# Turning the mixture's tokens and slot rows with VectorE and SBUF transfers instead of TensorE, and three PSUM copies on ScalarE

## The chip, the cores and the metric

The kernel runs on one core of a Trainium2 chip. A core has TensorE (PE in the profile; its weight loads are PEld), VectorE (DVE), ScalarE (ACT), GpSimd (POOL) and SyncE (SP), which here only starts transfers. Each engine works through its own list of instructions in order and waits on semaphores for the others. TensorE reads SBUF and writes PSUM, which has eight banks of 128 x 512 float32. The metric is the device time of one execution in microseconds; lower is better.

## The reference, cut to what matters

Tokens `x` of shape (2, 1024, 256), all in float32, pass four blocks, each added to `x`, with a parameterless layer norm in front:

```python
x = x + _L0_xattn_ref(_layernorm(x), ctx, Wq, Wk, Wv, Wo, bo)      # 8 heads, windowed, 64 context rows
x = x + _L0_ffn_ref(_layernorm(x), W1, b1, W2, b2)                 # 8 groups of tokens, no activation
x = x + _L1_xattn_ref(_layernorm(x), ctx, ctx, Wq, Wk, Wv, Wo)     # 16 heads, sigmoid scores
x = x + _L1_ffn_ref(_layernorm(x), gamma_x, gamma_slot, slot_embeds, w1, w2)
```

The last is a soft mixture with 1,024 slots. It is the part that most of the change touches:

```python
xn = rms_norm(x, gamma_x)
se = rms_norm(slot_embeds, gamma_slot)
logits = einsum('bsd,etd->bset', xn, se)
dispatch = softmax(logits, axis=1)          # over the tokens
slots = einsum('bsd,bset->betd', xn, dispatch)
processed = gelu(slots @ w1) @ w2
combine = softmax(logits over all slots)
out = einsum('bnd,bsn->bsd', processed, combine)
```

For the logits, both tokens and slot rows must lie with the 256 features on the partitions, that is, turned.

## The kernel before, in words

**Tiling.** The 2,048 tokens are four quads (`q` 0 to 3) of 512, each 4 tiles (`t`) of 128 tokens by 256 features, kept in SBUF as `xq[q]`. Quads 0 and 1 are sequence 0, quads 2 and 3 sequence 1. The 256 features are two halves of 128 (`c`, `dc`).

**Order.** The order on each engine is set at compile time: a scheduler reorders the program's instructions by its own estimates, and only the mixture's ScalarE instructions keep the written order. PSUM is two pools of four banks (`bank(name, side)`); a new bank waits until the one four earlier in its pool has been read out. So an instruction that reads a bank late can hold up TensorE four banks on.

**Layer 0** (L596 to L813). `weigh(q)` computes attention weights on VectorE and ScalarE, `attend(q)` turns them (`pat`, L760), copies them out of PSUM to `atT` (L762, on an engine that the compiler chooses) and multiplies (`po`, L767); VectorE adds that to `x` (L775). The feed-forward block has no activation, so `product(g)` multiplies its two weight matrices (`pmt`, L522), and `bias_rows(g)` sums the biases on VectorE, for `g` from 2 on as eight instructions of 128x256 (`b2z`, L553). `bias(g)` makes `bs` from them (`pbs`, L559; copied by L561), which GpSimd adds to `x` (L574); `norm_ff` and `feed_forward` finish (`hn_f` L486, `pt_f` L125, `hT_f` L126, `po` L580, L587).

**Layer 1** (L815 to L1006). Keys are masked by head parity out of PSUM bank `pk` (L862, VectorE), values copied from `pv` (L875, L885, VectorE). Then for each quad and each half `c` of the heads: scores (`psg`, L957), tanh on ScalarE (`sg`, L966), values (`poT`, L996; read out to `oT` by L1003). Between scores and values stands other work that hides ScalarE: the norm of the next quad (`hn_a` L486, turned by `pt_a` L125), its queries (`pq`, L897), and the output of the quad before (`pf`, L911; added to `x` by VectorE, L919).

**Mixture, preparation.** `norm_slots` scales the 1,024 slot rows `se`: squares on ScalarE (L826), the power on GpSimd (L829), three small steps on VectorE, and eight scalings on VectorE (L834). `turn_slot_rows(dc, h)` turns them on TensorE (`pse`, L842, four transposes each); VectorE copies them to `seT` and multiplies by both gammas on the way (L843). `norm_tokens(q)` computes moments (L113, L114), `rstd` and `f` (GpSimd L116, L117, L159, then six small VectorE steps L160 to L165) and `xh` (L169). `turn_tokens(q)` turns `xh` on TensorE (`pt_m`, L180, eight transposes), read out by ScalarE and VectorE (L150, L152) to `xhT`. `norm_tokens(0)` and `turn_tokens(0)` stand near the end of layer 1, the others among the logits.

**Mixture, logits and after** (L1012 on). For each row tile, `logits` multiplies `xhT` by `seT` (`pl`, L196); VectorE reads each 128x512 half twice (L204 for the negated logits and their minimum, L211 or L215 for the running maximum over tokens), ScalarE takes the exponential (L219). `largest` and `spread` bring the maxima to all partitions (`pm`, `pb`), GpSimd adds them (L278), ScalarE takes the second exponential (L281), and `gather`, `hidden`, `processed` and `combine` follow (L289, L364, L430, L455). `turn` (L228) already turns the combine weights `ec` without TensorE: VectorE turns 32x32 blocks (L236) and 16 transfers per piece (L243), issued by SP, put the blocks in their places.

Of the kernel before, what the change touches and what calls it, by code (L numbers as in the profile page):

```python
# [9 lines left out]
FP = mybir.dt.float32  # L10
AF = mybir.ActivationFunctionType
ALU = mybir.AluOpType
# [3 lines left out]
P = 128  # L16
B = 2
S = 1024
D = 256
DC = D // P  # L20
NK = 64
QT = 4
# [28 lines left out]
def tile_kernel(  # L51
# [9 lines left out]
    bo0: bass.AP,  # L61
    wff_in: bass.AP,
    b2: bass.AP,
    gammas: bass.AP,
    w1_in: bass.AP,
    slots_in: bass.AP,
# [12 lines left out]
    def bank(name, side=0):  # L79
        return ps[side].tile([P, 512], FP, tag="bank", name=name)  # L80
# [11 lines left out]
    nc.gpsimd.memset(m_half, -0.5)  # L92
    xq = [const.tile([P, QT, D], FP, name=f"x{q}") for q in range(NQ)]

    gxs = const.tile([P, 2, DC], FP, name="gxs")
    gx, gs = gxs[:, 0, :], gxs[:, 1, :]
    ggx = const.tile([P, DC], FP, name="ggx")

    parity = const.tile([P, 2], FP, name="parity")
    nc.vector.tensor_reduce(  # L100
# [2 lines left out]
        AX.XY,  # L103
        ALU.add,
    )
    seT = const.tile([P, DC, NSLOT], FP, tag="seT", name="seT")

    def moments(xt, name):

# [10 lines left out]
    def transposed(src, dst, name, side=0):  # L120

        for c in range(DC):
            pt = bank(f"pt_{name}_{c}", side)
            for t in range(QT):
                nc.tensor.transpose(pt[:, ts(t, P)], src[:, t, ts(c, P)], ident)  # L125
            nc.any.tensor_copy(dst[:, c, :], pt)  # L126


    outr = out.rearrange("(q t p) d -> q p t d", t=QT, p=P)
# [43 lines left out]
        xhs[q] = xh  # L173

    def turn_tokens(q):
        xhT = pools["mw"].tile([P, DC, QN], FP, tag="xhT", name=f"xhT_{q}", bufs=2)
        for c in range(DC):
            pt = bank(f"pt_m_{q}_{c}", 1)
            for t in range(QT):
                nc.tensor.transpose(pt[:, ts(t, P)], xhs[q][:, t, ts(c, P)], ident)  # L180
            copy(c, xhT[:, c, :], pt)
        xhTs[q] = xhT

    def logits(b, s):

        q, t = b * QB + s // QT, s % QT
        if s == 0:
            zcs[b] = stat.tile([P, ST], FP, tag="zc", name=f"zc_{b}")
            rmaxs[b] = pools["md"].tile([P, NSLOT], FP, tag="rmax", name=f"rmax_{b}")
        lg = keep[b].tile([P, NSLOT], FP, tag=f"lg_{s}", name=f"lg_{b}_{s}")  # L190
        lgs[b][s] = lg
        nm = stat.tile([P, 2], FP, tag="nm", name=f"nm_{b}_{s}")
        for n in range(NSLOT // 512):
            pl = bank(f"pl_{b}_{s}_{n}", 0)
            for dc in range(DC):
                nc.tensor.matmul(  # L196
                    pl,
                    lhsT=xhTs[q][:, dc, ts(t, P)],
                    rhs=seT[:, dc, ts(n, 512)],
                    start=(dc == 0),  # L200
                    stop=(dc == DC - 1),
                )

            nc.vector.tensor_tensor_reduce(  # L204
                lg[:, ts(n, 512)], pl, zero.to_broadcast([P, 512]), -1.0,
                BIG if n == 0 else nm[:, 0:1], ALU.add, ALU.min, nm[:, n : n + 1],
            )

            rm = rmaxs[b][:, ts(n, 512)]
            if s == 1:  # L210
                nc.vector.scalar_tensor_tensor(  # L211
                    rm, lgs[b][0][:, ts(n, 512)], -1.0, pl, ALU.mult, ALU.max
                )
            elif s > 1:
# [253 lines left out]
    with (  # L468
# [4 lines left out]
        wk1s, wv1s, wq1s, wo1s = (w1s[:, i] for i in range(4))  # L473
        se = w1p.tile([P, EC, D], FP, name="se")

        NCT, NPE = DC * 2 * B * NK, DC * NK
        fr = w1p.tile([P, NCT + NPE + NG * OC], FP, name="fr")
        ctxd = fr[:, 0:NCT].rearrange("p (c b e s) -> p c b e s", c=DC, b=B, e=2)
# [112 lines left out]
        def load_layer1():  # L591
            nc.sync.dma_start(out=w1s, in_=w1_in)
            nc.sync.dma_start(out=se, in_=slots_in)
            nc.sync.dma_start(out=gxs, in_=gammas)

        with tc.tile_pool(name="p0", bufs=1) as p0, tc.tile_pool(name="a0", bufs=2) as a0:  # L596

# [158 lines left out]
            def attend(q):  # L756
                atf = ats[q].rearrange("p g j -> p (g j)")
                pat = bank(f"pat_{q}")
                for t in range(QT):
                    nc.tensor.transpose(pat[:, ts(t, P)], atf[:, ts(t, P)], ident)  # L760
                atT = a0.tile([P, QN], FP, tag="atT", name=f"atT_{q}")
                nc.any.tensor_copy(atT, pat)  # L762
                for i in range(2):
                    po = bank(f"po0_{q}_{i}")
                    for k in range(2):
                        t = 2 * i + k
                        nc.tensor.matmul(  # L767
                            po[:, ts(k, D)],
                            lhsT=atT[:, ts(t, P)],
                            rhs=vw[:, (q * QT + t) // 2, :],  # L770
                            start=True,
                            stop=True,
                        )
# [41 lines left out]
        with (  # L815
# [4 lines left out]
            def norm_slots():  # L820
                sq = a1c.tile([P, D], FP, name="sq")
                sn = a1c.tile([P, EC], FP, name="sn")
                p_half8 = a1c.tile([P, EC], FP, name="p_half8")
                nc.gpsimd.memset(p_half8, 0.5)
                for c in range(EC):
                    nc.scalar.activation(  # L826
                        sq, se[:, c, :], AF.Square, accum_out=sn[:, c : c + 1]
                    )
                nc.gpsimd.tensor_tensor(sn, sn, p_half8, ALU.pow)  # L829
                nc.vector.tensor_scalar(sn, sn, RMS_EPS, None, ALU.max)  # L830
                nc.vector.reciprocal(sn, sn)
                nc.vector.tensor_scalar(sn, sn, float(D) ** 0.5, None, ALU.mult)
                for c in range(EC):
                    nc.vector.tensor_scalar(  # L834
                        se[:, c, :], se[:, c, :], sn[:, c : c + 1], None, ALU.mult
                    )
                nc.vector.tensor_tensor(ggx, gx, gs, ALU.mult)

            def turn_slot_rows(dc, h):
                pt = bank(f"pse_{dc}_{h}", 1)  # L840
                for c in range(4):
                    nc.tensor.transpose(pt[:, ts(c, P)], se[:, 4 * h + c, ts(dc, P)], ident)  # L842
                nc.vector.tensor_scalar(  # L843
                    seT[:, dc, ts(h, 512)], pt, ggx[:, dc : dc + 1], None, ALU.mult
                )

# [12 lines left out]
                    )  # L859
            for c in range(C1):  # L860
                for e in range(2):
                    nc.vector.tensor_scalar(  # L862
                        kblk[:, c, :, e, :],
                        pk[:, ts(c, P)].rearrange("p (b s) -> p b s", b=B),
                        parity[:, e : e + 1],
                        None,
                        ALU.mult,
                    )

            vblk1 = a1c.tile([P, B, H1 // 2, 2, DH1], FP, name="vblk1")  # L870
# [11 lines left out]
            pvv = pv.rearrange("p (b r e d) -> p b r e d", b=B, e=2, d=DH1)  # L882
            for e in range(2):
                r = slice(e * NK, (e + 1) * NK)
                nc.vector.tensor_copy(vblk1[r, :, :, e, :], pvv[r, :, :, e, :])  # L885

# [59 lines left out]
            )  # L946
            queries(0)
            bias(7)
            work = ExitStack()
            for q in range(NQ):  # L950
                b = q * QN // S
                oTs[q] = a1.tile([P, C1, QN], FP, tag="oT", name=f"oT_{q}")
                for c in range(C1):
# [15 lines left out]
                    if c == 0:  # L969
                        if q == 0:  # L970
# [4 lines left out]
                            pools["mw"] = work.enter_context(  # L975
                                tc.tile_pool(name="mw", bufs=1, reuse_waits="tile")
                            )
                            norm_slots()
                        if q + 1 < NQ:
                            hTs[q + 1] = layernorm(xq[q + 1], f"a1_{q + 1}", 1)  # L980
                        if q > 0:
                            output(q - 1, (0, 1) if q + 1 < NQ else (0,))
                            turn_slot_rows(*divmod(q - 1, 2))
                        if q + 1 == NQ:
                            turn_tokens(0)
                    elif q + 1 < NQ:
                        queries(q + 1)
                        if q + 2 == NQ:
                            norm_tokens(0)
                            turn_slot_rows(1, 1)  # L990
                    else:
                        output(q - 1, (1,))
                        logits(0, 0)
# [21 lines left out]
    for u in range(1, B * ST + 2):  # L1015
        b, s = divmod(u, ST)
        if b < B:
            if s % QT == 1:
                q = u // QT + 1
                if q < NQ:  # L1020
                    norm_tokens(q)
            logits(b, s)
            if s % QT == 2:
                q = u // QT + 1
                if q < NQ:
                    turn_tokens(q)
        v = u - ST
        if v == 1:
            nc.vector.reciprocal(zcs[0], zcs[0])
# [113 lines left out]
```

## Time and profile before

| what | us |
|---|---|
| median of three runs (461.42 to 462.01) | 461.6 |
| the profiled execution | 461.42 |
| its span in the trace | 459.6 |
| PE busy | 446.4 |
| DVE busy | 261.1 |
| ACT busy | 110.8 |
| POOL busy | 84.9 |

The profile is of one execution. Its page gives the busy time of each engine, the chain of work that ended last (at each step what released it), and the costliest groups of instructions by line. A timeline line gives the start, the duration, the engine, the line of the code, the operation, what is written from what, its shape, and in square brackets how long the engine had been idle and what ended that. Where several like instructions are merged into one line, the count stands behind x. A float32 matmul is two instructions in the trace. In the chain's own list the columns are start, length, and what.

### The profile page before, as it was taken

To read this page: it belongs to the slowest core of one execution; us is meant where nothing else is said; L and a number is where in the kernel's file an instruction comes from. 1 tells how busy PE (TensorE), PEld (TensorE's weight loads), DVE (VectorE), ACT (ScalarE), POOL (GpSimd) and SP (SyncE) were. 2 spreads that over 40 slices of the span, in tenths; PEclk is the share of its full clock that TensorE was granted. 3 is DMA by queue.
4 is the path that set the end of the run, shared out by engine and by line. 5 is a ranking of instruction groups with operands and counts; after the bars stand their busy time and mean duration, and the time that the engine had idled before them with its cause. 6 is when DMAs were issued, how large, how long until landed. Compare 5 with 4: busy or idle time off the path is not lost.

```text
span 459.6 us, 5446 instructions
## 1 busy us (share of the span) xinstructions
PE 446.4 (97%) x2032; PEld 322.2 (70%) x2032; DVE 261.1 (57%) x623; ACT 110.8 (24%) x205; POOL 84.9 (18%) x84
## 2 busy tenths in 40 slices
PE   6999897999999999999999999999999999999997
PEld 5788795888645555445458854688888874488886
DVE  0487889897256677987776279611331539911111
ACT  1212331211344441342573306300000003410000
POOL 3011332325111101100878910000000000000000
PEclk9999999999999999999999999999999999999999
DMA  8994691500000000000007534140252040430011
GB/s 287 411 429 198 260 427 45 185 0 1 1 1 0 2 0 1 0 0 1 0 1 227 89 52 72 33 80 0 52 98 36 12 79 1 82 102 1 11 47 35
DMA packets 74381, 38.61 MB, mean 84 GB/s; under 512 B 68465, under 2 KB 70641, under 8 KB 72945
## 3 DMA queue, kind: packets, MB, share of 16 engines
q1 hardware_dynamic: 74354, 38.26, 27.4%
q8 instruction: 16, 0.26, 0.2%
q14 instruction: 11, 0.09, 0.1%
HBM read 27.76 MB, written 2.10 MB: 65 GB/s over the span
## 4 chain that ended last, share of the span: by engine, by line
PE 82%; DVE 6%; POOL 1%; issue 0%
PE psl L289 12%; PE pc L455 12%; PE pp L430 12%; PE pl L196 11%; PE pmh L364 11%; PE pmt L522 6%; PE pq L897 3%; PE pf L911 3%; PE po L580 2%; PE psg L957 2%; PE poT L996 2%; DVE b2z L553 1%; DVE hn_f L486 1%; PE po L767 1%; PE pt_a L125 1%; PE pb L273 1%
## 5 line engine op out<-in xcount | busy, mean ns | idle before, releaser
L522 PE MATMUL pmt<-wg 128*128 128x256 f32 x256 | 60.1, 393 | 3.8 <-DMA wg<-in_wff_dram 3.8
L289 PE MATMUL psl<-xh,lg 128*128 128x258 f32 x256 | 58.7, 381 | 0.0
L522 PEld LDWEIGHTS pmt<-wg 128*128 128x128 f32 x256 | 49.9, 198 | 11.4 <-DMA wg<-in_wff_dram 4.3
L196 PE MATMUL pl<-seT,xhT 128*128 128x512 f32 x128 | 56.1, 592 | 0.0
L455 PE MATMUL pc<-pr,ec 128*128 128x256 f32 x256 | 55.6, 379 | 0.0
L430 PE MATMUL pp<-ms,mh 128*128 128x256 f32 x256 | 55.6, 379 | 0.0
L430 PEld LDWEIGHTS pp<-ms,mh 128*128 128x128 f32 x256 | 48.6, 190 | 7.5 <-DVE mh L408 0.5
L455 PEld LDWEIGHTS pc<-pr,ec 128*128 128x128 f32 x256 | 48.6, 190 | 6.6
L289 PEld LDWEIGHTS psl<-xh,lg 128*128 128x128 f32 x256 | 47.4, 190 | 7.2 <-issue 0.5
L196 PEld LDWEIGHTS pl<-seT,xhT 128*128 128x128 f32 x128 | 24.1, 190 | 27.9 <-issue 26.3
L278 POOL TENSOR_TENSOR lg<-lg,mb 128x1024 f32<-128x1024 f32 x16 | 37.2, 2366 | 32.3 <-ACT mb L150 27.9
L462 DVE SCALAR_TENSOR_TENSOR x<-pc,zc,x 128x256 f32<-128x256 f32 x16 | 7.7, 484 | 42.3 <-PE pc L455 42.3
L442 DVE COPY pr<-pp 128x512 f32<-128x512 f32 x8 | 5.5, 692 | 45.5 <-PE pp L430 45.5
L219 ACT ACTIVATE ec<-lg,nm 128x1024 f32<-128x1024 f32 x16 | 18.4, 1148 | 41.6 <-DVE nm L204 41.6
L398 ACT COPY mh<-pmh 128x512 f32<-128x512 f32 x8 | 4.6, 572 | 89.6 <-PE pmh L364 89.6
L374 ACT ACTIVATE mh<-mh 128x512 f32<-128x512 f32 x32 | 19.0, 626 | 21.1 <-DVE mh L408 16.1
L364 PE MATMUL pmh<-slT,ms 128*128 128x512 f32 x48 | 24.0, 592 | 0.0
L553 DVE SCALAR_TENSOR_TENSOR b2z<-wg,fr,b2z 128x256 f32<-128x256 f32 x48 | 23.6, 494 | 0.3
L297 DVE RECIPROCAL rz<-psl 128x1 f32<-128x1 f32 x16 | 2.6, 164 | 32.7 <-PE psl L289 32.7
L966 ACT ACTIVATE sg<-psg 128x512 f32<-128x512 f32 x32 | 16.5, 603 | 18.0 <-PE psg L957 18.0
L236 DVE STREAM_TRANSPOSE tr<-ec 128x512 f32<-128x512 f32 x32 | 20.1, 679 | 0.0
L281 ACT ACTIVATE lg<-lg 128x1024 f32<-128x1024 f32 x16 | 16.5, 1049 | 12.2 <-POOL lg L278 12.2
(169 smaller groups left out, 585.9 us busy)
## 6 DMA issues: line engine op xcount, KB each, us to landing
wg<-in_wff_dram SPq DMA_DIRECT2D x6, 2048.0 KB, 12.4
ec<-tr SPq DMA_DIRECT2D x128, 64.0 KB, 2.1
xT<-in_xT_dram SPq DMA_DIRECT2D x4, 512.0 KB, 13.4
x<-in_x_dram SPq DMA_DIRECT2D x4, 512.0 KB, 14.9
wg<-in_wff_dram SPq DMA_DIRECT2D x2, 1024.0 KB, 11.3
ms<-in_m_dram SPq DMA_DIRECT2D x1, 2048.0 KB, 8.3
out_dram<-x SPq DMA_DIRECT2D x16, 128.0 KB, 1.8
wg<-in_wff_dram SPq DMA_DIRECT2D x3, 512.0 KB, 6.0
```

The lines of the kernel that those rows point to most:

```text
L196: nc.tensor.matmul(pl, lhsT=xhTs[q][:, dc, ts(t, P)], rhs=seT[:, dc, ts(n, 512)], start=(dc == 0), stop=(dc == DC - 1),)
L219: nc.scalar.activation(ecs[q][:, :, t, :], lg.rearrange("p (h n) -> p h n", h=2), AF.Exp, bias=nm[:, 1:2], scale=-1.0, accum_out=zcs[b][:, ...
L236: nc.vector.transpose(tr[:, :, :, t, :].rearrange("p r c n -> p c r n"), half[:, t, :].rearrange("p (c r n) -> p c r n", c=EC // 2, r=R4),)
L278: nc.gpsimd.tensor_tensor(lgs[b][s], lgs[b][s], mbs[b], ALU.add)
L281: nc.scalar.activation(lgs[b][s], lgs[b][s], AF.Exp, scale=-1.0)
L289: nc.tensor.matmul(pz[:, 0:XW], lhsT=lgs[b][s][:, ts(c, P)], rhs=xhs[b * QB + s // QT][:, s % QT, :], start=(s == 0), stop=(s == ST - 1),)
L364: nc.tensor.matmul(to, lhsT=lefts[i][:, ts(j, P)], rhs=slTs[b][:, i, 0:512] if i < 2 else rights[b][i], start=True, stop=True,)
L374: nc.scalar.activation(h, h, AF.Gelu)
L430: nc.tensor.matmul(pp[:, ts(k, D)], lhsT=hss[b, g, fc // 2][:, fc % 2, ts(2 * c2 + k, P)], rhs=m12s[1][:, fc, :], start=(fc == 0), stop=(f ...
L455: nc.tensor.matmul(pc[:, 0:D], lhsT=turned[:, c // 4, c % 4, t, :], rhs=prs[b, c // 4][:, c % 4, :], start=(c == 0), stop=(c == EC - 1),)
L522: nc.tensor.matmul(pm[:, ts(hc, D)], lhsT=w1g[:, oc, ts(hc, P)], rhs=w2g[:, oc, :], start=(oc == 0 and hc == 0), stop=(oc == OC - 1 and hc ...
L553: nc.vector.scalar_tensor_tensor(acc, weights[g][1][:, oc, :], b1s[:, g, oc : oc + 1], acc, ALU.mult, ALU.add)
```

## The change

- A new function `turned` turns a quad-sized piece (4 tiles of 128x256): four VectorE 32x32-block transposes into a buffer `tr`, then 16 transfers of 32 KB within SBUF, issued by SP. `turn_tokens` and `turn_slot_rows` use it; their 48 TensorE transposes and the copies from PSUM are gone.
- The gammas are loaded a second time as rows spread over all partitions (`ggb`, 256 KB). GpSimd multiplies them together and multiplies the scaled slot rows by them, in two instructions of 128x1024. The scalings of the slot rows go from VectorE to ScalarE.
- `norm_slots` and the first half of the slot rows are written before the loop of layer 1, the second half in quad 0; `norm_tokens` and `turn_tokens` of quads 0 and 1 stand in the rounds of quads 1 and 2, those of quads 2 and 3 at the row tiles 1 and 3 of the logits. `xhT` has three buffers instead of two, and `seT` is laid out by slot half.
- The copies to `atT`, `kblk` (keys) and `vblk1` (values) are put on ScalarE.

```diff
+    def turned(src, dst, tr):
+        for t in range(QT):
+            nc.vector.transpose(
+                tr[:, :, :, t, :].rearrange("p r c n -> p c r n"),
+                src[:, t, 0:D].rearrange("p (c r n) -> p c r n", c=DC, r=R4),
+            )
+        to = dst.rearrange("p c (t i n) -> p (c t) i n", t=QT, i=R4)
+        for i in range(R4):
+            for r in range(R4):
+                nc.sync.dma_start(
+                    out=to[ts(r, SQ), :, i, :],
+                    in_=tr[ts(i, SQ), r].rearrange("p c t n -> p (c t) n"),
+                )
...
     def turn_tokens(q):
-        xhT = pools["mw"].tile([P, DC, QN], FP, tag="xhT", name=f"xhT_{q}", bufs=2)
-        for c in range(DC):
-            pt = bank(f"pt_m_{q}_{c}", 1)
-            for t in range(QT):
-                nc.tensor.transpose(pt[:, ts(t, P)], xhs[q][:, t, ts(c, P)], ident)
-            copy(c, xhT[:, c, :], pt)
+        xhT = pools["mw"].tile([P, DC, QN], FP, tag="xhT", name=f"xhT_{q}", bufs=3)
+        tr = pools["mw"].tile([P, R4, DC, QT, SQ], FP, tag="tr", name=f"tr_m_{q}", bufs=2)
+        turned(xhs[q], xhT, tr)
...
         def load_layer1():
             nc.sync.dma_start(out=w1s, in_=w1_in)
             nc.sync.dma_start(out=se, in_=slots_in)
-            nc.sync.dma_start(out=gxs, in_=gammas)
+            nc.sync.dma_start(out=gx, in_=gx_in)
+            nc.sync.dma_start(out=ggb, in_=gammas.partition_broadcast(P))
...
-                nc.any.tensor_copy(atT, pat)
+                nc.scalar.copy(atT, pat)
...
+                gg = ggb[:, 0, :]
+                nc.gpsimd.tensor_tensor(gg, gg, ggb[:, 1, :], ALU.mult)
                 for c in range(EC):
-                    nc.vector.tensor_scalar(
-                        se[:, c, :], se[:, c, :], sn[:, c : c + 1], None, ALU.mult
-                    )
-                nc.vector.tensor_tensor(ggx, gx, gs, ALU.mult)
+                    nc.scalar.activation(
+                        se[:, c, :], se[:, c, :], AF.Copy, scale=sn[:, c : c + 1]
+                    )
+                for h in range(2):
+                    sh = se[:, ts(h, QT), :]
+                    nc.gpsimd.tensor_tensor(
+                        sh, sh, gg.unsqueeze(1).to_broadcast([P, QT, D]), ALU.mult
+                    )
-            def turn_slot_rows(dc, h):
-                pt = bank(f"pse_{dc}_{h}", 1)
-                for c in range(4):
-                    nc.tensor.transpose(pt[:, ts(c, P)], se[:, 4 * h + c, ts(dc, P)], ident)
-                nc.vector.tensor_scalar(
-                    seT[:, dc, ts(h, 512)], pt, ggx[:, dc : dc + 1], None, ALU.mult
-                )
+            def turn_slot_rows(h):
+                tr = lnp.tile([P, R4, DC, QT, SQ], FP, tag="tr", name=f"tr_se_{h}")
+                turned(se[:, ts(h, QT), :], seT[:, h], tr)
...
-                    nc.vector.tensor_scalar(
+                    nc.scalar.activation(
                         kblk[:, c, :, e, :],
...
-                nc.vector.tensor_copy(vblk1[r, :, :, e, :], pvv[r, :, :, e, :])
+                nc.scalar.copy(vblk1[r, :, :, e, :], pvv[r, :, :, e, :])
...
             bias(7)
+            norm_slots()
+            turn_slot_rows(0)
...
-                            norm_slots()
...
                             output(q - 1, (0, 1) if q + 1 < NQ else (0,))
-                            turn_slot_rows(*divmod(q - 1, 2))
-                        if q + 1 == NQ:
-                            turn_tokens(0)
                     elif q + 1 < NQ:
                         queries(q + 1)
-                        if q + 2 == NQ:
-                            norm_tokens(0)
-                            turn_slot_rows(1, 1)
+                        if 0 < q:
+                            norm_tokens(q - 1)
+                            turn_tokens(q - 1)
+                        if q == 0:
+                            turn_slot_rows(1)
...
         if b < B:
-            if s % QT == 1:
-                q = u // QT + 1
-                if q < NQ:
-                    norm_tokens(q)
+            if u in (1, 3):
+                norm_tokens(QB + u // 2)
+                turn_tokens(QB + u // 2)
             logits(b, s)
-            if s % QT == 2:
-                q = u // QT + 1
-                if q < NQ:
-                    turn_tokens(q)
```

More of the change, by code (lines that the diff above doesn't have):

```diff
@@ L63, in tile_kernel @@
     b2: bass.AP,
+    gx_in: bass.AP,
     gammas: bass.AP,
@@ L93, in tile_kernel @@
     xq = [const.tile([P, QT, D], FP, name=f"x{q}") for q in range(NQ)]
-    gxs = const.tile([P, 2, DC], FP, name="gxs")
-    gx, gs = gxs[:, 0, :], gxs[:, 1, :]
-    ggx = const.tile([P, DC], FP, name="ggx")
+    gx = const.tile([P, DC], FP, name="gx")
     parity = const.tile([P, 2], FP, name="parity")
@@ L105, in tile_kernel @@
     )
-    seT = const.tile([P, DC, NSLOT], FP, tag="seT", name="seT")
+    seT = const.tile([P, 2, DC, 512], FP, tag="seT", name="seT")
     def moments(xt, name):
@@ L198, in logits @@
                     lhsT=xhTs[q][:, dc, ts(t, P)],
-                    rhs=seT[:, dc, ts(n, 512)],
+                    rhs=seT[:, n, dc, :],
                     start=(dc == 0),
@@ L474, in tile_kernel @@
         se = w1p.tile([P, EC, D], FP, name="se")
+        ggb = w1p.tile([P, 2, D], FP, name="ggb")
         NCT, NPE = DC * 2 * B * NK, DC * NK
@@ L861, in tile_kernel @@
                 for e in range(2):
-                    nc.vector.tensor_scalar(
+                    nc.scalar.activation(
                         kblk[:, c, :, e, :],
                         pk[:, ts(c, P)].rearrange("p (b s) -> p b s", b=B),
-                        parity[:, e : e + 1],
-                        None,
-                        ALU.mult,
+                        AF.Copy,
+                        scale=parity[:, e : e + 1],
                     )
@@ L1102 @@
     b1 = a["L0_ffn_b1"].reshape(NG, P, OC).transpose(1, 0, 2)
-    gxs = _np.stack([a["L1_ffn_gamma_x"], a["L1_ffn_gamma_slot"]]).reshape(2, DC, P)
+    gammas = _np.stack([a["L1_ffn_gamma_x"], a["L1_ffn_gamma_slot"]])
     laid = [
@@ L1119 @@
         ("b2", a["L0_ffn_b2"]),
-        ("gammas", gxs.transpose(2, 0, 1)),
+        ("gx", a["L1_ffn_gamma_x"].reshape(DC, P).T),
+        ("gammas", gammas),
         (
```

## The prediction

> **What bounds the kernel now.** I read the page's busy table first, then the chain that ended last, then the timeline of each engine around the places the change touches.
>
> ```profile
> PE 446.4 (97%) x2032; PEld 322.2 (70%) x2032; DVE 261.1 (57%) x623; ACT 110.8 (24%) x205; POOL 84.9 (18%) x84
> PE 82%; DVE 6%; POOL 1%; issue 0%
> 72.67 1.99 PE L767 MATMUL po<-vw,atT 128*128 128x256 f32 x8 [3.36 <-DVE atT L762]
> ```
>
> TensorE is busy for 446.4 of 459.6 us. From 72.67 us to the end the chain is nearly all TensorE. Before that VectorE sets the pace, and the one large hole late in it is the 3.36 us in front of L767, where `po` waits for a copy that stands in VectorE's queue. So a piece taken off TensorE after 72 us is worth its whole length, unless TensorE then arrives somewhere ahead of VectorE. I looked for such places in the compiled order of the changed kernel, engine by engine, and put the durations of this trace on it. A row's mean holds a tail that the next instruction overlaps, so I use the distance between starts: 0.33 us for a 128x256 VectorE instruction, 0.39 for a bias row (L553), 0.60 for 128x512, 0.31 and 0.09 for L113 and L114.
>
> **Term 1, the transposes: -5.2 us.** In the chain, eight `pt_m` transposes stand as 0.87 us and four `pse` as 0.44.
>
> ```profile
> 165.30 0.87 PE pt_m L180 x8
> 141.53 0.44 PE pse L842 x4
> ```
>
> Four of each go: 4 x 0.87 + 4 x 0.44 = 5.24. Their copies out of PSUM go too (L150 on ScalarE, L152 and L843 on VectorE).
>
> **Term 2, atT: -3.15 us at 72 us.** The last `pat` transpose ends near 67.9. TensorE then has six `pmt` pieces (to 69.14) and stops, because the copy is queued on VectorE:
>
> ```profile
> 69.75 0.68 DVE L587 TENSOR_TENSOR x<-x,po 128x512 f32<-128x512 f32 x1
> 71.94 0.68 DVE L762 COPY atT<-pat 128x512 f32<-128x512 f32 x1
> ```
>
> On ScalarE the compiled order has it behind four of the eight L826 squares (done at 64.9), so it ends at 68.5. What is late next is PSUM: the second half of L767 takes the bank that the L587 above frees at 70.43. TensorE runs 69.14 to 70.05, waits 0.4, and is through at 71.35 instead of 74.50. The other three atT copies are on ScalarE already.
>
> **Term 3, VectorE in front of layer 1: +3.2 us.** `pv` (L875) takes the bank that `bs` (L561, on VectorE) empties. Before, that is ready 4 us early:
>
> ```profile
> 103.85 0.39 DVE L561 COPY bs<-pbs 128x256 f32<-128x256 f32 x1
> 108.11 1.89 PE L875 MATMUL pv<-w1s,fr 128*128 128x256 f32 x8
> 92.16 1.36 DVE L486 TENSOR_SCALAR hn_a<-x,mv_a,rstd_a 128x256 f32<-128x256 f32 x1
> 91.81 1.56 POOL L574 TENSOR_TENSOR x<-x,bs 128x512 f32<-128x512 f32 x1 [1.13 <-ACT bs L561]
> L278 POOL TENSOR_TENSOR lg<-lg,mb 128x1024 f32<-128x1024 f32 x16 | 37.2, 2366 | 32.3 <-ACT mb L150 27.9
> L236 DVE STREAM_TRANSPOSE tr<-ec 128x512 f32<-128x512 f32 x32 | 20.1, 679 | 0.0
> ```
>
> The last four lines are the key. A VectorE instruction with its operands in SBUF that meets a wide GpSimd instruction ends only after it: `hn_a` took 1.36 instead of 0.41 and ended at 93.52, L574 at 93.37; a bias row at 81.39 took 1.50 in the same way. Stream transposes did not wait beside L278. The changed kernel puts two GpSimd products of 128x1024 (slot rows by gammas) among the last bias rows. The nearest row for them is L278, 2.37 us. The change from `bs` at 103.85: the atT copy and the waits about it bring VectorE 0.9 earlier to `sn`; eight L834 scalings leave (-2.1); eight 128x256 transposes come (8 x 0.33 = +2.6; the first group stands behind the first GpSimd product, the second behind the second); and three bias rows are held up, one by the L574 that GpSimd's new order puts behind `rstd_f` (+1.0), one by each new product (+2.0, +1.5). 103.85 - 0.9 - 2.1 + 2.6 + 4.5 = 107.95, ready at 108.2. TensorE would be at `pv` at 108.1 - 3.1 = 105.0, so it waits 3.2: the lead of term 2 is given back. Lower bound: bias rows are never held up, only the second transposes wait for the second product; `bs` is ready near 105.7 and ScalarE's eight scalings (8 x 0.32, ahead of two `hT_f` copies) hold `po` back 0.8 instead; the term is 0.8. Upper bound: transposes at the 128x512 row's 0.62, +5.5. I take 3.2, since two rows show the hold.
>
> The Trainium skill, "SBUF — State Buffer", section "Who interferes with whom", says that VectorE and GpSimd share a port pair as an exclusive lock for a whole instruction, for VectorE instructions with two SBUF inputs or in a two-port mode; this speaks against putting the gammas on GpSimd here. The longest hold in this trace is 1.1 us, of an instruction half as long as the new ones; with the hold capped at that the term would be 1.9 and the sum 459.9, by the page's whole instruction 3.2 and 461.2.
>
> **Term 4, second layer 1 quad: +3.5 us.** Before, `hn_a` of the last quad is computed at 131.69, long before its `pt_a` at 149.66. In the changed order its statistics are split around `x<-x,pf` and `oT`, its `rstd` is behind the mixture's three GpSimd steps, and two of its four pieces stand behind `xh` and the four new transposes.
>
> ```profile
> 131.69 1.38 DVE L486 TENSOR_SCALAR hn_a<-x,mv_a,rstd_a 128x256 f32<-128x256 f32 x4 [0.51 <-POOL rstd_a L117]
> 147.87 1.38 DVE L169 TENSOR_SCALAR xh<-x,mv_m,f 128x256 f32<-128x256 f32 x4
> 149.66 1.09 PE L125 MATMUL pt_a<-ident,hn_a 128*128 128x128 f32 x8
> ```
>
> On before's clock: last `mv_m` 144.3; GpSimd `rstd_m`, `f`, `rstd_m` to 146.6; last `mv_a` 147.45; `rstd_a` (1.47 from `mv` to `hn` before) gives the first `hn_a` at 148.95; one small `f`, one `hn_a`, four `xh` (1.3), four transposes (1.3), then the last two `hn_a`, at 153.1. `pt_a` ends at 153.8; TensorE without `pse` would have ended it at 150.3. Bounds: 2.3 (transposes free) to 4.7 (0.62 each).
>
> **Term 5, third quad: +1.0 us.** `xh` ends at 161.3, four transposes bring `oT` to 163.35, where before it was 163.2; TensorE is there 0.88 earlier (two `pse` gone). Bounds 0 to 2.2.
>
> **Term 6, first logits: +0.5 us.** Per 128x512 logits half VectorE needs 1.24 us (L204 and L211) of TensorE's 1.72. The norms of quads 2 and 3 now both fall in the first five row tiles, with four `xh` and four transposes (2.6) unbroken twice; the second time all four banks are full for about 0.5. Bounds 0 to 2.
>
> **What is hidden.** Six groups of 16 SBUF transfers go on SP's queue.
>
> ```profile
> ec<-tr SPq DMA_DIRECT2D x128, 64.0 KB, 2.1
> ```
>
> Those are issued every 0.63 us; the new ones hold 32 KB, so 16 x 0.63 + 2.1 = 12 us a group (bounds: 16 x 0.33, the shortest issue, to 16 x 1.1). The tightest, `xhT` of quad 0, starts near 152.5 and lands near 165; its first logits come near 172 with the waits above. SP has nothing behind them until `ms` at 241.94. The gammas' broadcast (256 KB) delays the next two FFN weights by 0.6; their traffic ends near 70 and TensorE needs them from 78. Keys and values: six copies on ScalarE, which idles 6 us there; needed from 111. Fewer products between `pb` and the first gathers: VectorE's and ScalarE's copies of `xhT`, which stood in front of `mb`, go too, and the last `dispatch` follows the last logits as before.
>
> **The sum**, against the profiled execution (461.42 us, 1.8 of it outside the span): -5.24 - 3.15 + 3.2 + 3.5 + 1.0 + 0.5 = -0.2, so 461.2. The median of the three runs is 461.6. A measurement tells about 0.2% (0.9 us) from no change: under 460.7 is faster, over 462.5 slower.
>
> The Trainium skill, "VectorE: DVE Perf Modes", section "The three transpose paths", gives VectorE 311 ns for a 128x128 transpose; as an estimate that is 0.62 us for each 128x256 here, and the sum would be 467. The row of L236 has 0.68 us for 128x512, four such blocks, and I go by the row.
>
> **The rivals.**
> 1. *The lead is kept* (0.27). The bias rows slip past the products, or VectorE is earlier: `bs` near 105.7, term 3 is 0.8. Time 461.2 - 2.4 = 458.8. For it: b2z rows are short and the products start only when ScalarE has scaled the rows. Against it: the second transposes stand behind the second product in any case.
> 2. *Slower, VectorE's transposes* (0.18). Price between the ends, 0.48 instead of 0.33 us: terms 3 to 6 hold 8 + 4 + 4 + 4 of them, +3.0 us, time 464.2. It decides from about 0.40, where the sum passes 462.5. For it: no row shows a transpose this short. Against it: at 0.62 for 512 columns L236 has no large fixed part.
> 3. *Slower, transfers late* (0.05). If a group takes 20 us instead of 12, the first logits wait for `xhT`; from then TensorE stands still, 1 to 3 us: 463.5.
> 4. *The work removed was hidden anyway* is within the forecast: without term 2 term 3 would vanish too.
>
> **Chances.** Forecast 0.50, own range 459.8 to 462.6, of which 0.28 lies under 460.7 and 0.12 over 462.5. Faster: 0.27 + 0.5 x 0.28 = 0.41. Slower: 0.18 + 0.05 + 0.5 x 0.12 = 0.29. Same: 0.30. The range takes in rival 1 with its lower bounds and rival 2: 457.6 to 464.4.
>
> **What would show it.** No `pt_m` or `pse`; `po` behind atT released at 70 by VectorE's L587; a TensorE wait of 2 to 3 us at `pv` ended by `bs`, with bias rows over 1.5 us beside the GpSimd products; one of about 3.5 at the last `pt_a`, one of about 1 at `pf` ended by `oT`; the 128x256 transposes at 0.33 to 0.35. I am wrong if `pv` does not wait, if the last `hn_a` is ready before its `pt_a`, or if logits wait for a transfer.

## The result, and the profile after

| | before | changed |
|---|---|---|
| median of 14 runs each (us) | 461.62 (461.01 to 462.51) | 463.29 (462.17 to 464.03) |
| the profiled execution (us) | 461.42 | 463.34 |
| its span (us) | 459.6 | 461.6 |
| PE busy (us) | 446.4 | 444.6 |

The ratio is 1.0032 (95% interval 1.0024 to 1.0041): slower by 0.3%, where the forecast was 0.1% faster. The time lies within the stated range, but on the side that had been given a chance of 0.29.

From the changed kernel's page, first the busy time of TensorE, then the granted TensorE clock in 40 slices of 11.5 us, then the shares of the chain that ended last:

```profile
span 461.6 us, 5510 instructions
...
PE 444.6 (96%) x1984; PEld 318.3 (69%) x1984; DVE 265.7 (58%) x624; ACT 113.9 (25%) x215; POOL 90.5 (20%) x87
...
PEclk9999999999999799999999999999999999999999
...
PE 69%; DVE 16%; POOL 3%; issue 1%; ACT 0%; ACTq 0%; POOLq 0%
```

Two things are to be seen. The chain has 13 points less TensorE and 10 more VectorE: TensorE now waits for VectorE in places where it did not. And one slice, from 150 to 162 us, has a clock of 7 tenths, where the row of the kernel before has a 9 in all 40.

Where TensorE stands still is read from its timeline (idle time and releaser in brackets). These are all its waits after 68 us; the `pf` line without a bracket is there for its length:

```profile
68.39 1.10 PE L785 MATMUL po<-vw,atT 128*128 128x256 f32 x4 [0.16 <-DVE x L604]
69.81 1.13 PE L785 MATMUL po<-vw,atT 128*128 128x256 f32 x4 [0.32 <-DVE x L604]
...
100.48 3.77 PE L597 MATMUL po<-mt,hT_f 128*128 128x256 f32 x16 [0.84 <-ACT hT_f L126]
...
107.21 1.99 PE L894 MATMUL pv<-w1s,fr 128*128 128x256 f32 x8 [1.64 <-DVE bs L578]
...
151.46 1.65 PE L125 MATMUL pt_a<-ident,hn_a 128*128 128x128 f32 x6 [2.59 <-DVE hn_a L503]
152.91 5.98 PE L930 MATMUL pf<-w1s,oT 128*128 128x256 f32 x16
...
168.15 1.56 PE L930 MATMUL pf<-w1s,oT 128*128 128x256 f32 x6 [0.87 <-DVE oT L1022]
...
241.69 1.98 PE L288 MATMUL pb<-dg,ones 128*128 128x512 f32 x4 [0.66 <-DVE dg L274]
```

The waits stand where the forecast put them (`po` at 70, `pv`, the last `pt_a`, `pf` of the third quad), and one more at `pb`. But sixteen `pf` pieces take 5.98 us at 152.91, and in the kernel before the same sixteen took 3.62:

```profile
150.59 3.62 PE L911 MATMUL pf<-w1s,oT 128*128 128x256 f32 x16
```

No line of the forecast has that. A table of the changed kernel in windows of 1 us points to the reason (in each line the window, its length, the busy time of PE, PEld, DVE, ACT and POOL, then the granted clock, the DMA share and GB/s):

```profile
149.00:150.00 1.00, 0.00 (x0) 0.00 (x0) 1.00 (x4) 1.00 (x3) 0.00 (x0) 1.00 0.00 0
150.00:151.00 1.00, 0.00 (x0) 0.00 (x0) 1.00 (x4) 0.30 (x1) 0.00 (x0) 0.93 0.00 0
151.00:152.00 1.00, 0.54 (x2) 0.40 (x3) 1.00 (x4) 0.00 (x0) 0.00 (x0) 0.50 0.00 0
...
156.00:157.00 1.00, 1.00 (x4) 0.82 (x3) 0.43 (x1) 0.00 (x0) 0.00 (x0) 0.50 0.42 63
157.00:158.00 1.00, 1.00 (x4) 0.80 (x4) 0.97 (x4) 0.00 (x0) 0.00 (x0) 0.66 0.24 35
158.00:159.00 1.00, 1.00 (x9) 0.59 (x11) 0.33 (x4) 0.00 (x0) 0.00 (x0) 1.00 0.44 65
```

TensorE stops at 148.9. About 2 us later the granted clock falls to 0.50, and it stays there to 157.6, long after work has come back. The SBUF transfers of the first quad begin in the same stretch (DMA share 0.2 to 0.4), so the two had to be told apart by experiment.

The ledger below takes the start of the same instruction in both traces. The offset is what TensorE is late (plus) or early (minus) in the changed kernel. Its first row has nothing to do with the change: it stands behind the first 32 `pmt` pieces, whose code is the same in both kernels, and which took 10.03 us in the trace of before and 9.02 in that of the changed kernel. The offset is still there, unchanged, in front of the atT copy:

```profile
67.85 1.46 PE L522 MATMUL pmt<-wg 128*128 128x256 f32 x6
66.76 1.46 PE L539 MATMUL pmt<-wg 128*128 128x256 f32 x6
```

In the profiled executions of all ten kernels the first `pp`, behind those 32 pieces, starts anywhere from 12.68 to 13.77 us, and at 13.05 and 13.50 in two (experiments 1 and 6) that share the changed kernel's code up to there. So the 1.1 us is scatter of the program's start.

| at | before | changed | offset | what lies in between |
|---|---|---|---|---|
| first `pp` | 13.77 | 12.68 | -1.09 | scatter of the start: -1.1 |
| `pmt` after `po` at 72 | 74.50 | 70.78 | -3.72 | term 2: -2.6 |
| `pt_a` after `pv` | 109.84 | 109.04 | -0.80 | term 3: +2.9 |
| `pf` of quad 0 | 137.91 | 136.84 | -1.07 | -0.3, small gaps of before gone |
| `pf` of quad 1 | 150.59 | 152.91 | +2.32 | one `pse` gone -0.5; term 4 +3.2; clock +0.7 |
| `poT` after it | 154.58 | 158.82 | +4.24 | one `pse` gone -0.5; clock +2.5 |
| second `poT` of the third quad | 166.10 | 169.64 | +3.54 | two `pse`, one `pt_m` gone -1.9; term 5 +1.2 |
| `pl` of the second row tile | 179.28 | 182.81 | +3.53 | |
| `psl` after `pb` | 241.64 | 243.51 | +1.87 | three `pt_m` gone -2.7; term 6 +1.0 |

The clock's share is 0.7 for six transposes (1.45 us to the next start, where six of before's eight in 0.93 take 0.70) and 2.5 for `pf` (5.91 against 3.46): 3.2 us together. The transposes (term 1) sum to -5.7. The terms: -1.1 - 5.7 - 2.6 + 2.9 - 0.3 + 3.2 + 3.2 + 1.2 + 1.0 = +1.8; the spans differ by 2.0. Without the start's -1.1 the sum is +2.9.

The ledger belongs to these two executions, and the medians differ by less, 1.7 us. Of the changed kernel's 14 executions five, the profiled one among them, had a mean granted clock of 0.992, the other nine 0.995 or 0.996, so that their clock was halved for a shorter time. In the median these nine were only 0.3 us shorter; what else set them apart is not known.

### The profile page after: what moved, and what is told of

It reads as the page before. It is cut to its first block, busy times and chain, and to the rows that moved or that the text cites. A ratio compares the mean times of both kernels' runs of the same rounds, so it can differ in the third digit from the quotient of the medians.

```text
span 461.6 us, 5510 instructions
## 1 busy us (share of the span) xinstructions
PE 444.6 (96%) x1984; PEld 318.3 (69%) x1984; DVE 265.7 (58%) x624; ACT 113.9 (25%) x215; POOL 90.5 (20%) x87
## 4 chain that ended last, share of the span: by engine, by line
PE 69%; DVE 16%; POOL 3%; issue 1%; ACT 0%; ACTq 0%; POOLq 0%
PE pc L470 12%; PE pp L445 12%; PE psl L304 11%; PE pl L211 11%; PE pmh L379 10%; DVE b2z L570 4%; PE pf L930 3%; DVE hn_f L503 2%; PE pq L916 2%; PE pmt L539 1%; DVE bn_a L113 1%; PE pt_a L125 1%; PE psg L978 1%; PE pb L288 1%; PE po L597 1%
## 5 line engine op out<-in xcount | busy, mean ns | idle before, releaser
L539 PE MATMUL pmt<-wg 128*128 128x256 f32 x256 | 59.0, 388 | 3.7 <-DMA wg<-in_wff_dram 3.7
L570 DVE SCALAR_TENSOR_TENSOR b2z<-wg,fr,b2z 128x256 f32<-128x256 f32 x48 | 27.0, 565 | 0.3
```

The source lines that it names most:

```text
L539: nc.tensor.matmul(pm[:, ts(hc, D)], lhsT=w1g[:, oc, ts(hc, P)], rhs=w2g[:, oc, :], start=(oc == 0 and hc == 0), stop=(oc == OC - 1 and hc ...
L570: nc.vector.scalar_tensor_tensor(acc, weights[g][1][:, oc, :], b1s[:, g, oc : oc + 1], acc, ALU.mult, ALU.add)
```

## The experiments

Theory A: the change would have paid about as forecast, but the new 2.59 us wait at `pt_a` made the clock fall, and that cost up to 3.2 us on top of the wait. Rival B: the transfers slow the matmuls. Rival C: the clock costs nothing, because VectorE's norm behind `pf` sets the pace. Beside these, terms 2 and 3 are tested by themselves. Line numbers shift by a few from kernel to kernel. All ratios are to the kernel before, run beside them, where its medians were 462.23 (first four) and 461.92 us (last four).

**1. Fill the wait.** In front of the last quad's transposes:

```diff
+    fill = []
+    FILL = 3
...
+            if name == "a1_3" and c == 0:
+                for k in range(FILL):
+                    nc.tensor.matmul(pt, lhsT=ident, rhs=fill[0], start=True, stop=True)
...
+        fill.append(w1s[:, 0].rearrange("p c d -> p (c d)"))
```

> The changed kernel with three 128x512 matmuls of no use put in front of the last quad's hn_a transposes in layer 1, so that TensorE works through most of the 2.59 us wait (148.87 to 151.46); their results are overwritten by the transposes. Theory A (clock): the granted clock was 0.50 from 150.9 to 157.6, after that wait, and made the six pt_a transposes left and sixteen pf pieces 3.1 us longer (1.45 for 0.8, 5.91 for 3.46). With TensorE busy the clock stays at 1.00, pf takes 3.5, the time is 463.3 - 3.1 = 460.2. Rival B (transfers): the first xhT transfers, which begin at 152.5, slow the matmuls; pf stays near 5.9 and the time near 463.3. Rival C: the clock is kept but VectorE's norm behind pf sets the pace, and the gain is given back as a longer wait for oT at the third quad: 462 to 463.

Measured: 460.89 us, ratio 0.9975 (0.9967 to 0.9983). TensorE's timeline:

```profile
148.59 2.84 PE L129 MATMUL pt_a<-w1s,ident 128*128 128x512 f32 x6
...
151.91 1.09 PE L131 MATMUL pt_a<-ident,hn_a 128*128 128x128 f32 x6 [0.26 <-DVE hn_a L510]
152.83 3.62 PE L937 MATMUL pf<-w1s,oT 128*128 128x256 f32 x16
```

The useful work starts no earlier than in the changed kernel (the six transposes at 151.91 against 151.46), the transfers run as before, and `pf` is back at 3.62 us. The granted clock was 1.00 to the end of the span. Useless work made the kernel 0.57% (2.6 us) faster, and turned slower than before into faster than before. Theory A holds; B falls, and so does C, since nearly all is kept. Of the 3.2 us that the ledger gives the clock, 2.6 come back by the ratios and 2.5 between the profiled executions (2.8 if the start, 0.4 us later in this one, is taken out).

**2. Remove the wait.** The last quad's layer norm ahead of the mixture norm of quad 0 (cut: `layernorm` is split, so that its first part, `normed`, can be called early):

```diff
+                        if q == 1:
+                            hns[3] = normed(xq[3], "a1_3")
                         if 0 < q:
                             norm_tokens(q - 1)
                             turn_tokens(q - 1)
```

> The changed kernel with the last quad's layer norm (statistics and hn_a) written ahead of the mixture norm of quad 0 on VectorE; nothing else is moved by hand. Theory A: the wait at pt_a goes (3.2 us against the kernel before's pace) and with it the half clock (3.1 us): 463.3 - 6.3 = 457.0; the wait for oT at the third quad stays at 0.9. Rival B (transfers slow the matmuls): pf stays near 5.9 us and only the wait goes: 460.1. Rival C: the norm and transposes of quad 1 set the pace behind pf and the third quad's wait for oT takes what is gained: 460 to 461.

Measured: 458.08 us, ratio 0.9913 (0.9900 to 0.9926).

```profile
148.49 1.09 PE L125 MATMUL pt_a<-ident,hn_a 128*128 128x128 f32 x8
149.42 3.92 PE L935 MATMUL pf<-w1s,oT 128*128 128x256 f32 x16
...
162.61 1.56 PE L935 MATMUL pf<-w1s,oT 128*128 128x256 f32 x6 [0.87 <-DVE oT L1029]
```

No wait at `pt_a`, a clock of 1.00, and the third quad's wait for `oT` is the same 0.87: nothing was given back there. The gain over the changed kernel is 1.0032 - 0.9913 = 1.19%, 5.5 us, where 6.3 was expected; `pf` takes 0.3 us longer than before, because its weight loads wait 0.44 us for `oT`. One reordered norm is worth about as much as all the transposes that the change takes off TensorE (5.7 us).

**3. One part alone: atT on ScalarE, in the kernel before.**

```diff
-                nc.any.tensor_copy(atT, pat)
+                nc.scalar.copy(atT, pat)
```

> The kernel before with one part of the change: the atT copy on ScalarE. Forecast's terms 2 and 3 taken apart: po starts 3.2 to 3.7 us earlier at 72 us, and without GpSimd's products and the new transposes in front of it bs is ready near 104, at or before TensorE's arrival at pv (104.4 to 105.0), so the gain is kept: 461.6 - 3.4 = 458.2. Rival: VectorE paces layer 1's start in any case and TensorE only waits later, at pv or at the norm in front of it; 460.8 or more.

Measured: 461.95 us, ratio 0.9999 (0.9990 to 1.0007). The expectation was wrong: the lead, 3.9 us at `pv` of which 0.8 stood at the program's start, was worth nothing. TensorE's timeline, and the VectorE line that releases it:

```profile
104.26 1.89 PE L875 MATMUL pv<-w1s,fr 128*128 128x256 f32 x8
105.99 1.04 PE L125 MATMUL pt_a<-ident,hn_a 128*128 128x128 f32 x8
109.78 8.63 PE L522 MATMUL pmt<-wg 128*128 128x256 f32 x32 [2.75 <-issue]
...
108.57 1.11 DVE L862 TENSOR_SCALAR kblk<-pk,parity 128x128 f32<-128x128 f32 x4
```

The lead is whole at `pv` (104.26 against 108.11). Then `pmt` waits 2.75 us. The profile puts it down to "issue", but the next bank of its pool is the one of `pk`, four banks earlier, and the keys' copies out of it end on VectorE at 109.7; experiment 5 tests that reading. The clock then halves here too (0.50 from 109.3 to 112.8), and the 32 pieces take 8.63 us instead of 7.07. So 36 us after the place where it was won, the lead goes into a wait for a bank and the clock.

**4. Leave out GpSimd's two products,** on top of experiment 2:

```diff
-                for h in range(2):
-                    sh = se[:, ts(h, QT), :]
-                    nc.gpsimd.tensor_tensor(
-                        sh, sh, gg.unsqueeze(1).to_broadcast([P, QT, D]), ALU.mult
-                    )
```

> The early-norm kernel (the last quad's layer norm ahead of the mixture norm) that leaves out the two GpSimd products of the slot rows with the gammas, so its logits lack the gammas. Theory (hold): bias rows took 2.00 and 2.21 us beside the products instead of 0.48, and the transposes waited for the second one; without them bs is ready near 103.5, the 1.64 us wait at pv goes, the 0.84 us wait for hT_f (eight scalings on ScalarE) stays: 457.0 - 1.6 = 455.4. Rival: the eight transposes and the order alone make bs late; the wait at pv shrinks by less than 0.4 and the time is 456.6 or more.

Measured: 455.90 us, ratio 0.9866 (0.9852 to 0.9880): 2.2 us less than experiment 2. First the changed kernel's timeline around the products, then this one's:

```profile
97.96 5.05 POOL L859 TENSOR_TENSOR se<-se,ggb 128x1024 f32<-128x1024 f32 x2 [1.01 <-ACT se L854]
...
98.81 2.00 DVE L570 SCALAR_TENSOR_TENSOR b2z<-wg,fr,b2z 128x256 f32<-128x256 f32 x1
100.73 0.43 DVE L134 STREAM_TRANSPOSE tr_se<-se 128x256 f32<-128x256 f32 x1
101.09 2.21 DVE L570 SCALAR_TENSOR_TENSOR b2z<-wg,fr,b2z 128x256 f32<-128x256 f32 x1
...
106.78 0.38 DVE L578 COPY bs<-pbs 128x256 f32<-128x256 f32 x1
```

```profile
98.90 0.48 DVE L575 SCALAR_TENSOR_TENSOR b2z<-wg,fr,b2z 128x256 f32<-128x256 f32 x1
99.30 0.44 DVE L134 STREAM_TRANSPOSE tr_se<-se 128x256 f32<-128x256 f32 x1
99.66 0.45 DVE L575 SCALAR_TENSOR_TENSOR b2z<-wg,fr,b2z 128x256 f32<-128x256 f32 x1
...
103.58 0.39 DVE L583 COPY bs<-pbs 128x256 f32<-128x256 f32 x1
```

The products end near 100.5 and at 103.0. Beside each a bias row lasts until the product is over (2.00 and 2.21 us), without them 0.45 to 0.48. `bs` comes 3.2 us earlier and the wait at `pv` is gone; the wait for `hT_f` behind ScalarE's eight scalings (0.85) stays. That is the hold of the forecast's term 3, near the 3.5 us that it had for the two products.

**5. All three ScalarE copies alone, in the kernel before.** As in experiment 3, and:

```diff
-                    nc.vector.tensor_scalar(
+                    nc.scalar.activation(
                         kblk[:, c, :, e, :],
...
-                nc.vector.tensor_copy(vblk1[r, :, :, e, :], pvv[r, :, :, e, :])
+                nc.scalar.copy(vblk1[r, :, :, e, :], pvv[r, :, :, e, :])
```

> The kernel before with all three copies of the change on ScalarE (atT, keys, values) and nothing else. In the run with atT alone TensorE came 3.9 us early to the last pmt group and waited 2.75 us there for the bank that the keys' copies on VectorE (108.57 to 109.6) empty, and the clock halved for 3.4 us. Theory: ScalarE empties that bank near 105, so the lead is kept: 3.9 us below the kernel before, near 458.0. Rival: the lead only moves on to a later VectorE wait (queries, or the layer norms of layer 1): less than 1.5 us is gained, 460.5 or more.

Measured: 457.78 us, ratio 0.9900 (0.9872 to 0.9927).

```profile
106.39 1.04 PE L125 MATMUL pt_a<-ident,hn_a 128*128 128x128 f32 x8
107.26 7.07 PE L522 MATMUL pmt<-wg 128*128 128x256 f32 x32
```

`pmt` follows without a wait, and the lead lasts to the end: 4.1 us between the medians, 3.7 between the spans of the profiled executions, of which 0.4 stood at the program's start. So the keys' and values' copies, which the forecast had at nothing, decide whether atT's move is worth nothing or 3.3 to 4.1 us. It also says what turning by VectorE and transfers did in the changed kernel: with the copies alone 0.9900, with everything 1.0032.

**6. How long a wait halves the clock.** As experiment 1, with one filling matmul instead of three.

> The changed kernel with one filling matmul of 128x512 (0.9 us) instead of three in front of the last quad's hn_a transposes: TensorE still stands still for some 1.7 us. If only waits near 2.6 us and more halve the clock (the 1.64 us wait at pv did not), the clock stays at 1.00 and the time is that of three matmuls, 460.9. If any wait over 1.5 us just behind the scores halves it, pf takes 5.9 and the time is near 463.

Measured: 461.05 us, ratio 0.9988 (0.9967 to 1.0009), and two kinds of execution: seven of twelve took 460.4 to 461.2 us with a mean clock of 0.999 or 1.000, five took 462.5 to 463.3 with 0.996. The profiled one is of the second kind (0.50 from 152.4 to 155.8):

```profile
152.30 1.65 PE L131 MATMUL pt_a<-ident,hn_a 128*128 128x128 f32 x6 [1.97 <-DVE hn_a L510]
153.74 4.71 PE L937 MATMUL pf<-w1s,oT 128*128 128x256 f32 x16
```

Neither expectation holds as written: with a wait of about 2 us (1.97 in the one profile) the clock falls in some executions and not in others of the same kernel. The medians of the two kinds, 463.05 and 460.76, put the price at 2.3 us.

**7. Put the slot rows where VectorE is idle.** On top of experiment 2: scaling and gammas in one VectorE instruction, into buffers that come free in layer 1's first quad. ScalarE's eight scalings and GpSimd's two products are left out, and both halves of the slot rows are turned in quad 0.

```diff
             def turn_slot_rows(h):
+                sh = lnp.tile([P, QT, D], FP, tag="hn", name=f"se_n_{h}")
+                for t in range(QT):
+                    c = h * QT + t
+                    nc.vector.scalar_tensor_tensor(
+                        sh[:, t, :], se[:, c, :], sn[:, c : c + 1], gg, ALU.mult, ALU.mult
+                    )
...
-                turned(se[:, ts(h, QT), :], seT[:, h], tr)
+                turned(sh, seT[:, h], tr)
```

> The early-norm kernel with the slot rows' scaling and gammas in one VectorE instruction of 128x256 per tile, into buffers that come free only in layer 1's first quad: the eight scalings on ScalarE, both GpSimd products and the eight transposes leave the place in front of bs. Theory (hold): bs is ready before 102, the waits for hT_f (0.84) and at pv (1.64) both go, and VectorE has room for 8 x 0.4 + 8 x 0.33 = 5.8 us in 113 to 136: 458.1 - 2.5 = 455.6. Rival: the lead is taken back by another wait before layer 1 (the bank of keys or values, the last weights) or by the slot rows in layer 1's first quad: 457 or more.

Measured: 455.39 us, ratio 0.9848 (0.9818 to 0.9878), the fastest here, 6.5 us below the kernel before between the medians.

```profile
101.83 0.39 DVE L583 COPY bs<-pbs 128x256 f32<-128x256 f32 x1
...
116.72 1.67 DVE L865 SCALAR_TENSOR_TENSOR se_n<-se,sn,ggb 128x256 f32<-128x256 f32 x4
118.31 1.42 DVE L134 STREAM_TRANSPOSE tr_se<-se_n 128x256 f32<-128x256 f32 x4
```

`bs` is out of the way, both waits in front of layer 1 are gone, and the slot rows' work stands from 116.7 to 122.8, where VectorE has room (in the kernel before it is busy for 2.6 of the 9 us from 116 to 125). Against experiment 5 the turned tokens and slot rows are now worth 0.9900 - 0.9848 = 0.52%, 2.4 us; the intervals just overlap.

**8. atT back on VectorE,** on top of experiment 2 (the reverse of experiment 3's edit).

> The early-norm kernel with the atT copy back on the engine that the compiler picks (VectorE, as before). Forecast's terms 2 and 3 say that the lead of atT is given back in front of layer 1: TensorE comes 3.7 us later to 72 us, but then does not wait for hT_f (0.84) and at pv (1.64), and bs comes up to 0.9 later: 458.1 + 0.8 to 1.8, near 459.2. Rival: the lead is not given back; 461.5.

Measured: 460.06 us, ratio 0.9952 (0.9936 to 0.9968), by the ratios 1.8 us more than experiment 2 and a little above what was expected.

```profile
72.86 2.43 PE L790 MATMUL po<-vw,atT 128*128 128x256 f32 x8 [3.71 <-DVE atT L785]
75.09 7.06 PE L544 MATMUL pmt<-wg 128*128 128x256 f32 x26
```

The waits for `hT_f` and at `pv` disappear, as the forecast said. But behind the wait of 3.71 us the clock is halved (0.50 from 74.3 to 77.6), and 2.43 and 7.06 us are 0.4 and 1.3 more than the 1.99 and 5.78 of the same pieces at full clock. That 1.7 is nearly the whole difference: with the clock apart, terms 2 and 3 do cancel in the changed kernel's order.

## Why the prediction was wrong

**What bounds the kernel**: right. TensorE carries the chain, and every place named as a new wait became one, except the logits of term 6.

**Term 1** (forecast -5.2): right, -5.7. The instructions are gone; counted to the next start, the small gaps around them go too.

**Term 2** (-3.15): right in mechanism, 0.5 too large: -2.6 from the same start. `po` waits 0.16 and 0.32 us behind VectorE's `x<-x,po`, where the forecast had one such wait of 0.4; that instruction comes 0.4 us later than assumed, because the `hn_f` in front of it took 2.73 us instead of 2.33. Experiment 3 has a lead of 3.0 by the same count.

**Term 3** (+3.2): right in size (+2.9) and in mechanism, by experiment 4. It came in two pieces. 0.84 us is `hT_f` behind ScalarE's eight scalings, which the forecast had only in its lower bound; `bs` was then 1.64 us late instead of 3.2. The Trainium skill, "SBUF — State Buffer", section "Who interferes with whom", says that a VectorE instruction with two SBUF inputs contends with a GpSimd instruction that reads SBUF, over a port pair that is an exclusive lock; the 2.00 and 2.21 us agree. The cap at 1.1 us that the forecast weighed against it was wrong.

**Term 4** (+3.5): the wait was right, +3.2, for the reason given: two `hn_a` stand behind `xh` and the new transposes on VectorE.

```profile
148.40 1.38 DVE L187 TENSOR_SCALAR xh<-x,mv_m,f 128x256 f32<-128x256 f32 x4
149.69 1.42 DVE L134 STREAM_TRANSPOSE tr_m<-xh 128x256 f32<-128x256 f32 x4
151.03 0.70 DVE L503 TENSOR_SCALAR hn_a<-x,mv_a,rstd_a 128x256 f32<-128x256 f32 x2
```

**Here the prediction failed.** It priced the wait at its length, and took the work behind it at the durations of before: "`pt_a` ends at 153.8". The clock fell during the wait, and 22 instructions behind it took 3.2 us more. That one missing term is larger than the distance between 461.2 and 463.3, and experiment 1, which keeps the clock up and leaves the useful work as late as it was, gives 460.9. The profile of before misled on it: it has a wait of 3.36 us at 69.3 and a clock of 1.00 in every slice.

**Term 5** (+1.0): right, +1.2; the wait for `oT` is 0.87 us.

**Term 6** (+0.5): the size was near (+1.0), the place wrong. The logits wait for nothing. The microsecond is lost at 241.69, behind `dg`, which takes 2.24 us instead of 1.23 (two lines of before, two of the changed kernel):

```profile
226.71 11.65 POOL L278 TENSOR_TENSOR lg<-lg,mb 128x1024 f32<-128x1024 f32 x5
238.45 1.23 DVE L259 TENSOR_TENSOR dg<-ident,mT 128x1024 f32<-128x1024 f32 x1
...
228.90 11.64 POOL L293 TENSOR_TENSOR lg<-lg,mb 128x1024 f32<-128x1024 f32 x5
239.40 2.24 DVE L274 TENSOR_TENSOR dg<-ident,mT 128x1024 f32<-128x1024 f32 x1
```

GpSimd's products run to 240.5, 2.2 us later than in the kernel before, so that `dg`, with two SBUF inputs, now meets the last of them. That looks like the hold of term 3 once more, at a place that the forecast did not look at; no run tests it.

**What is hidden**: the transfers were (as an estimate, a group of 16 issued every 0.61 us that lands 2.0 us later takes 15 x 0.61 + 2.0 = 11.2 us), and no wait of TensorE is put down to one. The keys' and values' copies cost nothing, as forecast, but they decide what atT's move is worth (experiments 3 and 5). The forecast asked what `bs` would hold up four banks on, and not what `kblk` would.

**The rivals**: the lead kept did not happen. VectorE's transposes as the price on the slower side did not either: they start 0.34 us apart (1.42 us for four, 0.41 for one), about as forecast. The estimate of 0.62 us beside it did not hold; the figure behind it is one for bf16, and the data here is float32. The slower side came by a mechanism that no rival had.

**The sum**: -0.2 was forecast. Without the clock and the scatter of the start the ledger has -0.3, with the clock +2.9. That the rest agrees so well is partly luck: single terms were off by 0.2 to 0.5 us in both directions.

## What to carry to other kernels

Where a change adds a wait on TensorE of about 2 us or more, price it as the wait and, behind it, the chance of 3 to 7 us at half speed, which cost 1.7 to 3.2 us here; then look whether an order removes the wait, or whether useless work can fill it. A copy taken off a late engine is only worth its lead if every later reader that frees a bank is early as well: follow the lead bank by bank to the end before it is booked. Wide two-input work on GpSimd should not stand beside VectorE's own two-input work where TensorE waits for the latter (experiment 4); moving it elsewhere on GpSimd was not tried.

## What the runs showed of the hardware

- Waits of TensorE and the granted clock. The lengths are those of the one profiled execution of each kernel, the counts are of all its executions by their mean clock (0.992 to 0.996 where it fell, 0.999 or 1.000 where it did not). With a wait of 2.59 us the clock fell in 14 of 14 executions, with one of 1.97 in 5 of 12, with one of 2.75 us in 10 of 11, with one of 3.71 in 12 of 12. With none longer than 1.63 us it fell in none of 16 (experiments 1 and 2).
- Length alone does not decide. The wait of 3.36 us in the profiled execution of before left the clock at 1.00. Of that kernel's other executions beside the experiments, 19 of 23 and 18 of 23 had a mean clock of 0.996 or less, but these were only 0.7 and 0.4 us longer in the median than the rest; where in them the clock fell no profile shows. Nor does the fall always come in the wait: it came 2.0 to 2.3 us after TensorE stopped in the changed kernel and in experiments 3 and 6, but 5.1 us after it in experiment 8, where TensorE had been at work again for 1.4 us. And a full clock does not make every execution short: the one of experiment 3 that kept it took 462.89 us, the longest of the eleven, for a reason that no profile shows.
- The half clock lasted 3.3 to 3.4 us (experiments 3, 6 and 8) or 6.7 us (the profiled execution of the changed kernel). The Trainium skill, "TensorE: Matmul & The Clock Gate", section "Part 1: The HAM clock gate (the "warmup" mystery)", has a free-running window of 3.4 us, which fits these lengths, one or two of them, and the mixture in experiment 6; no run tests it. Its section "HAM oscillation — how this bites in real kernels" warns of gaps over about 3.4 us; here the clock fell every time behind a wait of 2.59 us, so the measurement decides. Whether the light 32-row score matmuls in front of that wait help to trip it was not tried.
- A VectorE transpose of 128x256 was not held up beside GpSimd's second product: 0.43 us at 100.73, where the bias row behind it took 2.21.
